# A gated recurrence on one core: the product of z of half B with chunk 0 of h moved in front of the first product with h of half B

## The chip, the cores and the metric

The kernel runs on one core of one Trainium2 chip. The metric is the device time of one execution in microseconds (us). The engines are called as the profile calls them: PE is TensorE with its products, PEld its weight loads, DVE is VectorE, ACT is ScalarE, POOL is GpSimd and SP is SyncE.

## The reference

A recurrence over 512 time steps, for 8 sequences, with a state h of 512 units; x has 512 units per step as well. Cut to what matters:

```python
def step(h, x_t):
    fused = sigmoid(concatenate([x_t, h], axis=-1) @ w_W + w_b)      # 1024 -> 1024
    hidden_state, output_state = split(fused, 2, axis=-1)            # r and z
    memory_state = x_t @ wx_W + wx_b + hidden_state * (h @ wh_W + wh_b)
    h_new = output_state * h + (1.0 - output_state) * tanh(memory_state)
    return (h_new, h_new)
_, hs = scan(step, cond_1024, swapaxes(x, 0, 1))
return x + swapaxes(hs, 0, 1)
```

Everything is float32. In the kernel, r is the gate `hidden_state`, z is the gate `output_state`, "h" is the product of h with `wh_W`, and n is the tanh.

## The kernel before, in words

The 512 units of the state are held as four chunks of 128 partitions by 8 sequences. Chunks 0 and 1 are half A, chunks 2 and 3 half B. The state of half A is in the tiles hTA, that of half B in hTB. Each of them holds a group of 4 steps (GS) in 32 columns, of which the columns of the present step are in use and the others are zero.

What a step multiplies with h is 512x1536 weights: wh, r and z, for 512 outputs each. The outputs lie 32 units (strips, index j) at a time on the partitions of PSUM, as 4 strips of 32 partitions, so that one weight load of TensorE is 128x32 of the state, and the products of the four strips stand beside each other in the array. The columns of the outputs are divided over three banks: A (192 columns: wh, z and r of half A), Z (64 columns: z of half B) and B (128 columns: r and wh of half B). For each bank there are four products, one per chunk k of h, and each is four matmuls (j = 0 to 3). So "A2" is the product of chunk 2 with the columns of bank A. In the trace every matmul stands as two weight loads and two products, 8 of each for an item such as A2. There are two sets of banks, one for the group of 4 steps in work and one for the next. Inside a group the banks gather: the rows of the steps are apart, so each step adds to its own rows.

The order of the items is written out by hand in ORDER (L20) and read in the loop over the 512 steps, just ahead of the rest of a step; the kernel is under a manual schedule there, so each engine works in the order of the text. Products A0, A1, B0, B1, Z0 and Z1 read hTA; A2, A3, B2, B3, Z2 and Z3 read hTB.

After the twelve items of a step comes one item of `prefill`: four matmuls of 384 columns of wx with x of a later group (xp in the profile), which are not part of the recurrence. They go into the bank xp, which is started from the bias by `seed`; ScalarE copies (`spread`, L169) carry it to the banks of the next group in the first and second step of a group, and VectorE turns the part for n (`turn_x`, L172) in the third. The last 8 steps have no such item.

The rest of a step is on VectorE and ScalarE, in this order on VectorE: turn r of half A (`tr`, the first to read bank A, L223), turn wh of half A (`md`, L235), turn z of half A (`tz`, L223), memory of half A (`m`, L252), turn wh of half B (first to read bank B), z times h of half A (`kept`, hd1A, L263), turn r of half B, update of half A (hTA, L275), turn z of half B (`tz` from bank Z), memory of half B, kept of half B, update of half B (hTB). ScalarE makes the sigmoids and tanhs between them (L145). GpSimd adds x to the new state for the output (L308), SyncE issues the loads of x and the stores of the output, one each in 16 steps.

So a step closes on itself in two ways: bank A, then VectorE and ScalarE, then hTA, then A0 of the next step; and bank A, VectorE and ScalarE, hTB, then A2 of the next step.

Of the kernel before, what the change touches and what calls it, by code (L numbers as in the profile page):

```python
# [16 lines left out]
HU = 64  # L17
SYNC = mybir.DependencyInfo(mybir.DependencyClass.Sync, mybir.DependencyReason.DATA)

ORDER = "A0 B0 A1 A2 A3 B1 B2 B3 Z0 Z1 Z2 Z3"  # L20

WH = {"A": slice(0, 192), "Z": slice(192, 256), "B": slice(256, 384)}

# [4 lines left out]
def tile_cond_rnn_residual(  # L28
# [165 lines left out]
    for i in range(T):  # L194
# [8 lines left out]

        for n in ORDER.split():
            bank, k = n[0], int(n[1])
# [175 lines left out]
```

## Time and profile before

| what | value |
|---|---|
| median of 3 runs | 1774.58 us (1774.36 to 1774.95) |
| the profiled execution, its own time | 1775.63 us |
| its span in the trace | 1773.9 us |
| granted TensorE clock | 0.998 |
| busy: PE, PEld, DVE, ACT, POOL | 1751.6, 1422.4, 1129.7, 857.4, 253.4 us |
| instructions in the trace | 121405 |
| products on PE, weight loads on PE | 53312 each |
| product of a bank-A item, mean of one | 327 ns (hTA), 340 ns (hTB) |
| product of a bank-B item, mean of one | 273 ns |
| product of a bank-Z item, mean of one | 223 ns (hTA), 225 ns (hTB) |
| product of the xp item, mean of one | 486 ns |

The means of one product contain its drain, and the products of a strip of four lie over each other, so the time that an item takes from the stream is not the sum of its means. It is read from the starts of the items in the timeline.

The longest waits in the trace are of GpSimd for hTA (1038.0 us in all) and of ScalarE for VectorE's first turn (723.6 us); neither engine is busy for half of the span. The DMA queues moved 31.11 MB in the span, 18 GB/s in the mean.

In the profile's lines, `A<-wh,hTA` is a product into bank A with a weight load from hTA; `128x192 f32 x8` are its partitions, columns, type and the number of instructions that were merged in a line. What stands in square brackets is the idle time of the engine before it and what ended this.

### The profile page before, as it was taken

To read this page: it belongs to the slowest core of one execution; us is meant where nothing else is said; L and a number is where in the kernel's file an instruction comes from. 1 tells how busy PE (TensorE), PEld (TensorE's weight loads), DVE (VectorE), ACT (ScalarE), POOL (GpSimd) and SP (SyncE) were. 2 spreads that over 40 slices of the span, in tenths; PEclk is the share of its full clock that TensorE was granted. 3 is DMA by queue.
4 is the path that set the end of the run, shared out by engine and by line. 5 is a ranking of instruction groups with operands and counts; after the bars stand their busy time and mean duration, and the time that the engine had idled before them with its cause. 6 is when DMAs were issued, how large, how long until landed. Compare 5 with 4: busy or idle time off the path is not lost.

```text
span 1773.9 us, 121405 instructions
## 1 busy us (share of the span) xinstructions
PE 1751.6 (99%) x53312; PEld 1422.4 (80%) x53312; DVE 1129.7 (64%) x6274; ACT 857.4 (48%) x4610; POOL 253.4 (14%) x1053
## 2 busy tenths in 40 slices
PE   7999999999999999999999999999999999999998
PEld 5888888888888888888888888888888888888887
DVE  2666666666666666666666666666666666666665
ACT  2444444444454444444444444444444444444444
POOL 1111111111111111111111111111111111111111
PEclk9999999999999999999999999999999999999999
DMA  4000000000000000000000000000000000000000
GB/s 174 16 4 16 16 16 16 6 15 16 17 16 16 4 16 17 16 16 5 16 16 16 16 15 5 16 16 16 17 4 16 16 16 16 4 16 11 10 10 10
DMA packets 11236, 31.11 MB, mean 18 GB/s; under 512 B 1361, under 2 KB 1361, under 8 KB 10705
## 3 DMA queue, kind: packets, MB, share of 16 engines
q1 hardware_dynamic: 10704, 23.35, 3.9%
q8 instruction: 416, 6.82, 1.6%
q14 instruction: 116, 0.94, 0.2%
HBM read 14.96 MB, written 8.39 MB: 13 GB/s over the span
## 4 chain that ended last, share of the span: by engine, by line
PE 95%; DVE 2%; DMA 1%; ACT 1%; issue 1%; SPq 0%; POOLq 0%; DVEq 0%; POOL 0%; ACTq 0%
PE A L131 40%; PE B L131 24%; PE xp L131 18%; PE Z L131 13%; DMA hin<-in_h_dram 1%; DVE tr L223 1%; DVE hTA L275 0%; ACT md0A L145 0%; DVE m L252 0%; DVE hd1A L263 0%; DMA wx<-in_wx_dram 0%; DVE hTB L275 0%; ACT zB L145 0%; DVE tz L223 0%; DVE md L235 0%
## 5 line engine op out<-in xcount | busy, mean ns | idle before, releaser
L131 PE MATMUL A<-wh,hTA 128*32 128x192 f32 x8192 | 527.1, 327 | 11.2 <-DVE hTB L120 7.4
L145 ACT ACTIVATE md0A<-tr 128x16 f32<-128x16 f32 x512 | 120.9, 236 | 723.6 <-DVE tr L223 723.6
L131 PE MATMUL A<-wh,hTB 128*32 128x192 f32 x8192 | 455.5, 340 | 2.1 <-DVE hTB L275 1.5
L131 PEld LDWEIGHTS A<-wh,hTA 128*32 128x32 f32 x8192 | 275.8, 137 | 220.7 <-DVE hTA L275 212.5
L223 DVE STREAM_TRANSPOSE tr<-A 128x64 f32<-128x64 f32 x512 | 127.9, 250 | 479.9 <-PE A L131 479.9
L131 PE MATMUL xp<-wx,xin 128*32 128x384 f32 x4096 | 425.9, 486 | 0.0
L131 PE MATMUL B<-wh,hTA 128*32 128x128 f32 x8192 | 414.8, 273 | 0.0
L131 PEld LDWEIGHTS A<-wh,hTB 128*32 128x32 f32 x8192 | 273.2, 142 | 105.3 <-DVE hTB L275 98.9
L131 PEld LDWEIGHTS B<-wh,hTA 128*32 128x32 f32 x8192 | 325.2, 136 | 10.3
L131 PE MATMUL B<-wh,hTB 128*32 128x128 f32 x8192 | 318.3, 273 | 0.0
L308 POOL TENSOR_TENSOR ot<-xin,hTA 128x16 f32<-128x16 f32 x512 | 125.8, 246 | 1127.2 <-DVE hTA L275 1038.0
L131 PEld LDWEIGHTS B<-wh,hTB 128*32 128x32 f32 x8192 | 248.3, 136 | 0.0
L131 PE MATMUL Z<-wh,hTB 128*32 128x64 f32 x8192 | 222.6, 225 | 0.0
L131 PE MATMUL Z<-wh,hTA 128*32 128x64 f32 x8192 | 217.2, 223 | 0.0
L131 PEld LDWEIGHTS Z<-wh,hTA 128*32 128x32 f32 x8192 | 200.9, 141 | 0.0
L131 PEld LDWEIGHTS Z<-wh,hTB 128*32 128x32 f32 x8192 | 182.1, 147 | 0.0
L308 POOL TENSOR_TENSOR ot<-xin,hTB 128x16 f32<-128x16 f32 x512 | 124.3, 243 | 389.6 <-DVE hTB L275 389.6
L145 ACT ACTIVATE md0B<-tr 128x16 f32<-128x16 f32 x512 | 119.2, 233 | 108.0 <-DVE tr L223 106.6
L275 DVE TENSOR_TENSOR_SCAN hTB<-hd0B,hd1B 128x32 f32<-128x32 f32 x512 | 115.1, 225 | 55.0 <-DVE hd1B L263 1.0
L235 DVE STREAM_TRANSPOSE md<-B 128x64 f32<-128x64 f32 x512 | 146.7, 286 | 0.6 <-issue 0.5
L235 DVE STREAM_TRANSPOSE md<-A 128x64 f32<-128x64 f32 x512 | 135.8, 265 | 0.0
L252 DVE TENSOR_TENSOR_SCAN m<-md0B,md 128x32 f32<-128x32 f32 x512 | 133.8, 261 | 0.5
(42 smaller groups left out, 1767.3 us busy)
## 6 DMA issues: line engine op xcount, KB each, us to landing
xin<-in_x_dram SPq DMA_DIRECT2D x32, 256.0 KB, 3.0
out_dram<-ot SPq DMA_DIRECT2D x32, 256.0 KB, 2.1
wx<-in_wx_dram SPq DMA_DIRECT2D x4, 768.0 KB, 6.6
wh<-in_wh_dram SPq DMA_DIRECT2D x4, 768.0 KB, 13.5
bias<-in_bias_dram SPq DMA_DIRECT2D x4, 64.0 KB, 2.0
hin<-in_h_dram SPq DMA_DIRECT2D x1, 16.0 KB, 15.0
```

What stands on the lines that cost most here:

```text
L131: nc.tensor.matmul(out_, lhsT, rhs, start=start, stop=False, skip_group_check=True)
L145: inst = nc.scalar.activation(*args, **kw).ins
L223: nc.vector.transpose(t_.rearrange("p c n -> p (c n)"), raw[n][hf])
L235: nc.vector.transpose(md1[g % 2][:, hf, :, :, 0].rearrange("p n c -> p c n"), raw["h"][hf])
L252: nc.vector.tensor_tensor_scan(flat(m), flat(md0[hf][g % 2][:, rows]), flat(md1[g % 2][:, hf, rows]), 0.0, ALU.mult, ALU.add,)
L275: nc.vector.tensor_tensor_scan(flat(hT[hf][(i + 1) % NH][:, B * s1 : B * s1 + B]), flat(hd0[hf][i % 2]), flat(hd1[hf][i % 2]), 0.0, ALU.mu ...
L308: inst = nc.gpsimd.tensor_tensor(ot[:, 2 * hf : 2 * hf + 2, t, :].rearrange("p c n -> p n c"), xins[c][:, 2 * hf : 2 * hf + 2, t * B : t * ...
```

## The change

One line: Z0, the product of chunk 0 of h (half A) with the columns of z of half B, goes from behind B3 to a place in front of A2, the first item that reads hTB.

```diff
-ORDER = "A0 B0 A1 A2 A3 B1 B2 B3 Z0 Z1 Z2 Z3"
+ORDER = "A0 B0 A1 Z0 A2 A3 B1 B2 B3 Z1 Z2 Z3"
```

In the program that is built from it, the four matmuls of Z0 stand between those of A1 and those of A2 in each step. The first of them now carries a wait of its own: for VectorE (its reading of bank Z in the step before) or, in the first step of a group, for ScalarE (its copy into bank Z). Before, VectorE's was contained in the wait of A2. The lists of instructions of VectorE and ScalarE are the same, line by line.

## The prediction

> **What bounds the kernel now.** I read the busy shares first, then the waits, then the timeline of one step, because a busy share near one hides the stalls that matter here. The page's first part says:
>
> ```profile
> PE 1751.6 (99%) x53312; PEld 1422.4 (80%) x53312; DVE 1129.7 (64%) x6274; ACT 857.4 (48%) x4610; POOL 253.4 (14%) x1053
> ```
>
> TensorE looks full. But a product counts as busy while it drains, so the 99% cannot tell a full stream from one with short holes. The view of waits names the holes (who waited, for whom, us in total, times, longest):
>
> ```profile
> DVE tr L223 <- PE A L131: 479.9, 512, 3.3
> PEld A L131 <- DVE hTA L275: 212.5, 509, 1.5
> PEld A L131 <- DVE hTB L275: 98.9, 499, 0.6
> ```
>
> Twice in each of 512 steps a weight load waits for the new state (hTA, then hTB), and VectorE's first turn of a step waits for bank A. So there is a loop through both engines. Which is longer, loop or stream? The timeline of one undisturbed step (start, length, engine):
>
> ```profile
> 903.66 0.83 PE L131 MATMUL xp<-wx,xin 128*32 128x384 f32 x8
> ...
> 904.20 0.27 PEld L131 LDWEIGHTS A<-wh,hTA 128*32 128x32 f32 x8 [0.40 <-DVE hTA L275]
> ...
> 904.30 0.51 PE L131 MATMUL A<-wh,hTA 128*32 128x192 f32 x8
> ...
> 904.63 0.40 PE L131 MATMUL B<-wh,hTA 128*32 128x128 f32 x8
> ...
> 904.85 0.51 PE L131 MATMUL A<-wh,hTA 128*32 128x192 f32 x8
> ...
> 904.92 0.23 DVE L275 TENSOR_TENSOR_SCAN hTB<-hd0B,hd1B 128x32 f32<-128x32 f32 x1
> 905.20 0.54 PEld L131 LDWEIGHTS A<-wh,hTB 128*32 128x32 f32 x16 [0.19 <-DVE hTB L275]
> 905.20 0.89 PE L131 MATMUL A<-wh,hTB 128*32 128x192 f32 x16
> ...
> 905.90 0.40 PE L131 MATMUL B<-wh,hTA 128*32 128x128 f32 x8
> ...
> 906.15 0.25 DVE L223 STREAM_TRANSPOSE tr<-A 128x64 f32<-128x64 f32 x1 [1.01 <-PE A L131]
> ...
> 907.30 0.22 DVE L275 TENSOR_TENSOR_SCAN hTA<-hd0A,hd1A 128x32 f32<-128x32 f32 x1
> 907.44 0.22 DVE L223 STREAM_TRANSPOSE tz<-Z 128x64 f32<-128x64 f32 x1
> 907.58 0.27 PEld L131 LDWEIGHTS A<-wh,hTA 128*32 128x32 f32 x8 [0.40 <-DVE hTA L275]
> ...
> 908.30 0.22 DVE L275 TENSOR_TENSOR_SCAN hTB<-hd0B,hd1B 128x32 f32<-128x32 f32 x1
> ...
> 908.58 0.22 PEld L131 LDWEIGHTS A<-wh,hTB 128*32 128x32 f32 x8 [0.18 <-DVE hTB L275]
> ```
>
> Here is A0 (904.30), B0, A1, then A2 and A3 (905.20), which need hTB, then the B products. A2's load goes from 905.20 to 908.58: 3.38 us, the step. Finer numbers are medians of record starts over steps 100 to 499, in ns.
>
> - **The PE stream.** Unstalled, an A item takes 325, a B item 218, the four Z items 113, 124, 123 and 124, xp 645. Sum 1300+872+484+645 = 3301.
> - **Loop B.** From A2's load to the end of A3's issue 706 (905.20 to 905.90), drain until tr starts 250 (906.15), VectorE and ScalarE until hTB is written 2371 (908.52), then 53 to the load: 3380.
> - **Loop A.** From hTA's end to A0's load 53; A0, B0, A1, A2, A3 on the array 325+218+325+650 = 1518; drain 250; tr to hTA's end 1371 (906.15 to 907.52). A late load also costs its own time: when A2's load comes late, A2 takes 379 to the next item instead of 325, so the array starts about 56 after its load. Sum 53+56+1518+250+1371 = 3248.
>
> The median period is 3383, so loop B binds; the stream has 80 to spare and loop A 132. Cross-check: A1 to A3 starts take 350+379 = 729 instead of 650, a stall of 79, which is the stream's spare time; A0's load stands 110 ahead of its product where 56 would do, 54 more, and 79+54 = 133 is loop A's.
>
> **What the Trainium skill says.** "Perfetto Trace Analysis", Identifying the Most-Contended Engine: matmul busy time is a poor measure, because matmuls are pipelined. The trace agrees: 99% busy over a stall of 79 ns per step. "TensorE: Matmul & The Clock Gate", Step-by-step: what each phase is for: weight loads may be pulled ahead of running products while products stay in order. It agrees: B0's load starts 161 ns ahead of its product. The same page, LDWEIGHTS: a load takes about columns/1.2 ns, 27 ns for 32 columns; the trace shows 56 from a late group of four loads to effective work, and I use 56. "TensorEngine Tiling (Array Packing)", Instruction Overhead: about 60 cycles for any product, so that short ones gain nothing by being shorter. The Z item of 113 to 124 against 218 for twice the columns shows at most a small floor.
>
> **The change, part by part.** Instruction counts, durations and the order on VectorE, ScalarE, GpSimd and SyncE stay; no DMA moves. Four matmuls of 64 columns (eight loads and eight products in the trace) go from after B3 to before A2.
>
> - *Removed behind B3:* one Z item, 118 (113 to 124). From A3's issue to the end of xp it was 654+484+645 = 1783, now 1665. This takes nothing off the time, because A0 will wait for hTA: after A3's issue hTA takes 250+1371, and A0 can start 109 later, at 1730. A pause of 65 opens before A0.
> - *Added before A2:* the same item. It fills the 79 in which the array now waits for hTB. Loop A becomes 3248+118 = 3366 (3361 to 3372), the stream stays 3301, loop B stays 3380: it starts at A2's load, and nothing between there and the next hTB moves relative to it, except that Z1 to Z3 and xp come earlier. The stall goes from the eye but not from the loop: about 14 remain before A2. Cost 0, covered by loop B with 14 ns.
> - *Z's end:* tz of Z comes 118 nearer to being safe. In the waits VectorE never waits for PE there; it follows hTA at once. Gain 0.
> - *An added wait:* Z0 now waits itself for VectorE's tz of the step before (and in the first step of a group for ScalarE's copy). Queued behind it on PE are A2 and all the rest, and VectorE's tr waits for A3. tz ends at 907.66; Z0 comes 868 after 907.69, so the wait has been over for about 0.9 us. A passed wait has no price in the trace: Z0 carried the ScalarE wait in one step of four and came at 2251 there, 2252 in others. I take 0.
> - *Z0's price in its new place* is not shown by the trace, since it always follows B products. Low end 113, the fastest Z item; high end 124+56 = 180, if it or A2 can't have its weights loaded under the product before. I take 118, because A1's second half lasts 162 and covers the load just as B3's 109 does. The high end costs (3248+180-3380) x 511 periods = 24.5 us; the low end can't gain, since loop B doesn't contain the item.
> - *First step:* nothing waits for hTB there, so A3 is 0.12 us later, once.
> - *Late VectorE instructions:* in some 55 places one comes 0.16 to 0.36 us late, 13 us altogether. Both loops pass through VectorE, so such a delay counts once, before and after. Carrying the three sums through all steps with each step's own VectorE times gives 0.1 us more.
>
> Sum: +0.2 us on the profiled execution's 1775.63 (span 1773.9, 1.7 around it): 1775.8. The median of the runs is 1.05 below it, so I say 1774.8.
>
> **The rivals.**
> *Faster: the hTB stall is real time that comes back.* For it: PE at 99%, and a wait of 98.9 us that Z0 covers. Against: loop B has no Z0. Were loop B shorter than it looks (a wait for bank Z in it, which now ends earlier), loop A would bind at 3366: 14 x 511 = 7.2 us, 1767.4. Chance 0.10.
> *Slower: hTA takes over.* Loop A grows past loop B when Z0 costs over 132 in place. Halfway into a reload, 118+28 = 146: 14 x 511 = 7.2 us, 1782.0; fully 1799. For it: the cover is only 14 ns, and A0 is now always late with its load. Against: in the disturbed steps where hTA was late A0 lost only 54, as counted. Chance 0.26.
> *Unchanged: loop B binds before and after.* 1774.8, chance 0.64.
> A measurement of this kernel can tell about 0.2%, 3.5 us, from no change; that is 7 ns per step, so Z0 up to 139 is "same".
>
> **How the numbers follow.** 0.64 within 0.2%, 0.26 slower, 0.10 faster. The forecast's own range is 1773.5 to 1777. The wide one goes down to 1772.5, leaving out most of the faster case (0.08), and up to 1783, where Z0 costs 148, leaving out the worse half of the slower one (0.11).
>
> **What would show it.** If right: A2's load to A2's load stays 3.38 us; A0's record to B0's becomes 379 instead of 325, A0's load just ahead of its product; VectorE's tr to hTB stays 2.37 us; the wait for hTB shrinks well below 98.9 us, although no time is gained; that for hTA grows by some 30 us. If A1 to A2 shows over 325+132, or A2's load comes well after hTB's write, the slower rival holds. If tr to hTB gets shorter than 2.37, the faster one does. The prediction is wrong if bank or memory contention between xp, now 118 ns earlier, and VectorE's turns alters the 2371.

## The result, and the profile after

| kernel | median | ratio to the kernel before on the same chip, 95% interval |
|---|---|---|
| before | 1774.73 us (12 runs) | |
| after | 1773.81 us (12 runs, 1773.11 to 1774.21) | 0.9994 (0.9985 to 1.0003) |

No difference that the measurement can tell. The profiled execution of after took 1773.73 us, its span is 1771.9 us. The first part of its page:

```profile
PE 1747.9 (99%) x53312; PEld 1448.8 (82%) x53312; DVE 1129.2 (64%) x6274; ACT 857.7 (48%) x4610; POOL 253.4 (14%) x1053
```

TensorE is as "full" as before. The waits of after show what moved (who waited, for whom, us in total, times, longest):

```profile
DVE tr L223 <- PE A L131: 478.3, 512, 3.5
...
PEld A L131 <- DVE hTA L275: 275.6, 511, 0.9
...
PEld A L131 <- DVE hTB L275: 2.9, 12, 0.3
```

The wait for hTB went from 98.9 to 2.9 us, and that for hTA from 212.5 to 275.6. VectorE waits for bank A as long as before (479.9 and 478.3). One row has nearly vanished from the view of waits, and the time is the same. The timeline of one step of after (start, length, engine) shows why:

```profile
903.79 0.56 PE L131 MATMUL A<-wh,hTA 128*32 128x192 f32 x8
...
904.17 0.40 PE L131 MATMUL B<-wh,hTA 128*32 128x128 f32 x8
...
904.51 0.23 DVE L275 TENSOR_TENSOR_SCAN hTB<-hd0B,hd1B 128x32 f32<-128x32 f32 x1
904.56 0.32 PEld L131 LDWEIGHTS Z<-wh,hTA 128*32 128x32 f32 x8
904.72 0.29 PE L131 MATMUL Z<-wh,hTA 128*32 128x64 f32 x8
904.79 0.54 PEld L131 LDWEIGHTS A<-wh,hTB 128*32 128x32 f32 x16
...
905.50 0.40 PE L131 MATMUL B<-wh,hTA 128*32 128x128 f32 x8
...
905.75 0.25 DVE L223 STREAM_TRANSPOSE tr<-A 128x64 f32<-128x64 f32 x1 [1.01 <-PE A L131]
...
906.51 0.83 PE L131 MATMUL xp<-wx,xin 128*32 128x384 f32 x8
...
906.89 0.23 DVE L275 TENSOR_TENSOR_SCAN hTA<-hd0A,hd1A 128x32 f32<-128x32 f32 x1
...
907.17 0.22 PEld L131 LDWEIGHTS A<-wh,hTA 128*32 128x32 f32 x8 [0.53 <-DVE hTA L275]
...
908.17 0.54 PEld L131 LDWEIGHTS A<-wh,hTB 128*32 128x32 f32 x16
```

Z0 (904.72) stands where TensorE stood still. A2's load goes from 904.79 to 908.17, 3.38 us, as before. The load follows the end of hTB (904.51+0.23 = 904.74) by 0.05, as before: it still waits for hTB, but the loads of Z0 (904.56, for 0.32 us) now run until past its start, so that the view no longer counts an idle engine. The pause has moved to the front of A0: its load (907.17) came 0.10 ahead of its product before and comes with it now, and A0 takes 0.38 to B0 (903.79 to 904.17) where it took 0.33.

### The profile page after: what moved, and what is told of

It is laid out like the page before. It is cut to its first block, busy times and chain, and to the rows that moved or that the text cites. A ratio compares the mean times of both kernels' runs of the same rounds, so it can differ in the third digit from the quotient of the medians.

```text
span 1771.9 us, 121405 instructions
## 1 busy us (share of the span) xinstructions
PE 1747.9 (99%) x53312; PEld 1448.8 (82%) x53312; DVE 1129.2 (64%) x6274; ACT 857.7 (48%) x4610; POOL 253.4 (14%) x1053
## 4 chain that ended last, share of the span: by engine, by line
PE 94%; DVE 3%; DMA 1%; ACT 1%; issue 1%; SPq 0%; DVEq 0%; POOLq 0%; POOL 0%
PE A L131 40%; PE B L131 24%; PE xp L131 17%; PE Z L131 13%; DMA hin<-in_h_dram 1%; DVE tr L223 1%; DVE hTA L275 1%; ACT md0A L145 0%; DVE m L252 0%; DVE hd1A L263 0%; DMA wx<-in_wx_dram 0%; DVE md L235 0%; DVE hTB L275 0%; DVE tz L223 0%; ACT zB L145 0%
## 5 line engine op out<-in xcount | busy, mean ns | idle before, releaser
L131 PE MATMUL A<-wh,hTA 128*32 128x192 f32 x8192 | 549.3, 340 | 13.5 <-DVE hTB L120 7.5
L131 PEld LDWEIGHTS A<-wh,hTA 128*32 128x32 f32 x8192 | 247.9, 142 | 283.8 <-DVE hTA L275 275.6
L131 PE MATMUL A<-wh,hTB 128*32 128x192 f32 x8192 | 437.6, 331 | 1.4
L223 DVE STREAM_TRANSPOSE tr<-A 128x64 f32<-128x64 f32 x512 | 127.9, 250 | 478.3 <-PE A L131 478.3
L131 PE MATMUL Z<-wh,hTA 128*32 128x64 f32 x8192 | 305.5, 220 | 0.0
L131 PEld LDWEIGHTS Z<-wh,hTA 128*32 128x32 f32 x8192 | 297.1, 136 | 6.0
L235 DVE STREAM_TRANSPOSE md<-B 128x64 f32<-128x64 f32 x512 | 142.9, 279 | 0.6 <-issue 0.6
```

The lines of the kernel that those rows point to most:

```text
L131: nc.tensor.matmul(out_, lhsT, rhs, start=start, stop=False, skip_group_check=True)
L223: nc.vector.transpose(t_.rearrange("p c n -> p (c n)"), raw[n][hf])
L235: nc.vector.transpose(md1[g % 2][:, hf, :, :, 0].rearrange("p n c -> p c n"), raw["h"][hf])
```

## The experiments

The period is the median time from one A0 to the next over steps 100 to 499; other numbers in ns are medians over the same steps. Each ratio is to the kernel before on the same chip. Three readings had to be told apart. *Loop*: the period is the longest of loop A (through hTA), loop B (through hTB) and the PE stream (all products of a step, one behind the other); loop B binds before and after. *Stream*: PE at 99% is full, so order can't matter. *Compensation*: the stall before A2 was real time that the change won, and hTA, now late, gave the same back by chance.

**Two items of Z in front of A2.**

```diff
-ORDER = "A0 B0 A1 A2 A3 B1 B2 B3 Z0 Z1 Z2 Z3"
+ORDER = "A0 B0 A1 Z0 Z1 A2 A3 B1 B2 B3 Z2 Z3"
```

> Z0 and Z1 both stand in front of A2. Loop theory (the period is the longest of loop A through hTA, loop B through hTB, and the PE stream): from the trace after, loop A with Z0 is 325+218+325+113+650 on the array, 251 drain, 1369 to hTA, 54 to the load, 56 for it = 3361 ns; Z1 adds 124, 3485. That is 105 over loop B (3380): 105 x 511 = 53.7 us, so 1828 us (1824 to 1833), and hTB no longer waited for. Stream theory (PE is full, order does not matter): 1774, no change. Compensation theory (hTA already binds after the change, by chance at the old length): +124 x 511 = 63 us, 1837.

Measured: 1831.2 us, ratio 1.0317 (1.0302 to 1.0333). The period is 3491 ns, for 3485 expected. From the waits of this kernel:

```profile
PEld A L131 <- DVE hTA L275: 341.1, 511, 1.2
```

That is 65 us more than in after, and the wait of A2's load for hTB, 2.9 us in after, is down to 0.2. Stream falls: the work on PE is the same and the time is 3% longer. The second Z item cost 113 ns per step (3491 against 3378 in after) of the 124 that it takes.

**Another filler, B1 in front of A2.**

```diff
-ORDER = "A0 B0 A1 A2 A3 B1 B2 B3 Z0 Z1 Z2 Z3"
+ORDER = "A0 B0 A1 B1 A2 A3 B2 B3 Z0 Z1 Z2 Z3"
```

> The order of before with B1, instead of Z0, in front of A2: another filler of 218 ns. Loop theory: loop A 3248+218 = 3466 ns, 86 over loop B; 86 x 511 = 44 us, so 1819 us (1814 to 1822). Stream theory: 1774.7, no change. Compensation theory (the filler takes the 79 ns of stall and gives back what is over 79, then 79 more because A0 is late): anything from +31 to +71 us, 1806 to 1846.

Measured: 1817.82 us, ratio 1.0242 (1.0227 to 1.0257), period 3466 ns. B1 takes 218 ns where loop A had 132 to spare, and 83 more per step are paid, for 86 expected. So it is the length that counts, and not the bank.

**hTB made early, on the order of before.** Half B takes the gates r and z of half A, so that hTB no longer waits for its own; these are computed and not read.

```diff
-                flat(md0[hf][g % 2][:, rows]),
+                flat(md0[0][g % 2][:, rows]),
...
-                zs[hf][i % 2].rearrange("p c n -> p n c"),
+                zs[0][i % 2].rearrange("p c n -> p n c"),
...
-                flat(hd0[hf][i % 2]),
+                flat(hd0[0][i % 2]),
...
-        turn_z(1)
         memory(1)
         kept(1)
+        turn_z(1)
         update(1)
```

> The order of before, but half B takes r and z from half A (its own are still turned and still go through the sigmoid, but nobody reads them, and the turn of z of half B stands behind kept of half B): hTB no longer waits for them. Product and state of half B are therefore not the reference's. All instructions stay, hTA's path stays; hTB comes about 230 ns earlier, loop B 3150. Loop theory: the PE stream binds, 3301 ns, 80 under the period of before: 80 x 511 = 41 us less, and part of the 13 us of late VectorE instructions is covered as well: 1734 us (1722 to 1737). Stream theory: 1774.7, no change, since PE's work is the same.

Measured: 1731.08 us, ratio 0.9754 (0.9738 to 0.977), period 3307 ns. From tr to hTB it is 1997 ns now, 374 less than the 2371 of before (I had expected some 230), and the way from tr to hTA is as before (1370). Still the period stops at 3307: that is the PE stream, estimated at 3301, and no item comes late any more (A0 to B0, A1 to A2 and A2 to A3 are 325 each). The load of A0 still waits for hTA, 206.4 us in all, but it is 101 ns ahead of its product, so this wait costs nothing. PE's page row reads 99% here too:

```profile
PE 1709.7 (99%) x53312; PEld 1493.7 (86%) x53312; DVE 1015.4 (59%) x6274; ACT 904.8 (52%) x4610; POOL 254.1 (15%) x1053
```

The same 53312 products at the same share of the span, 43 us shorter: the 99% of before was not a full stream.

**The same edit on the order of after.** Against the kernel of the experiment above:

```diff
-ORDER = "A0 B0 A1 A2 A3 B1 B2 B3 Z0 Z1 Z2 Z3"
+ORDER = "A0 B0 A1 Z0 A2 A3 B1 B2 B3 Z1 Z2 Z3"
```

> The same edit to the order of after (half B takes r and z from half A, its own are computed and not read). Loop theory: now loop A binds at 3361 ns, only 17 under the period after: 17 x 511 = 9 us less than 1773.8, and a few us of late VectorE instructions after hTA: 1764 us (1758 to 1767), 30 us above the same edit on the order of before. Stream theory: no change, and no difference between the two orders. Compensation theory (hTA binds already after the change): 1773.8, no change, with the order of before at 1734.

Measured: 1763.13 us, ratio 0.9933 (0.9918 to 0.9948), period 3366 ns. Compensation falls: with hTB out of the way after gains 12 ns per step (3378 to 3366), so hTB had been binding in after as well. (The mean gains 19, the time 11 us: the steps with a late VectorE instruction got cheaper too.) And the two orders that are alike by the clock differ by 32 us as soon as loop B is short.

**Without the products of x**, which are left out from the third group on, on the order of before.

```diff
-            pre = prefill(g + 2) if g + 2 < NG else iter(())
+            pre = iter(())
```

> The order of before without the xp items in the loop (the products of x with wx are left out from the third group on, so that only the bias and h's products enter there). PE's stream falls from 3301 to 2656 ns per step. Loop theory: loop B stays 3380 ns and binds, 1774 us (1771 to 1777), with TensorE visibly idle about 0.7 us in each step. Stream theory: 645 x 504 steps = 325 us less, 1450 us; or, if only its 80 ns stall shows, at least 40 us less.

Measured: 1772.01 us, ratio 0.9988 (0.9981 to 0.9995). Its page:

```profile
PE 1564.9 (88%) x49280; PEld 1348.9 (76%) x49280; DVE 1125.6 (64%) x6274; ACT 856.8 (48%) x4610; POOL 252.8 (14%) x1053
```

And the start of a step in its timeline:

```profile
906.01 0.56 PE L131 MATMUL A<-wh,hTA 128*32 128x192 f32 x8 [0.35 <-DVE hTA L275]
```

645 ns of product time taken from each step of 3383 bring 2 us in all; the period is 3375. TensorE's work is not the bound. The 0.7 us of visible idle time that I had expected are 0.35: by the starts of the items the stream has 3375-2656 = 719 ns to spare, but the view counts the last Z product as busy for about 0.2 us after the next item could start, and shows no hole before A2 and behind late loads.

**Z0 elsewhere in front of A2.**

```diff
-ORDER = "A0 B0 A1 A2 A3 B1 B2 B3 Z0 Z1 Z2 Z3"
+ORDER = "A0 Z0 B0 A1 A2 A3 B1 B2 B3 Z1 Z2 Z3"
```

> Z0 directly behind A0 instead of directly ahead of A2: the same items ahead of A2, in another order. Loop theory: loop A is the same sum, 3361 ns, loop B binds, the same time as after, 1773.8 us (1772.5 to 1775.5); it does not matter where in front of A2 the item stands. A theory in which Z0's place next to A2's late load, or its own wait for the turn of z, decides its price: a difference of over 10 ns per step, 5 us, either way.

Measured: 1773.86 us, ratio 0.9998 (0.999 to 1.0007), period 3379 ns for after's 3378. The trace agrees more closely than the time, in which loop B hides up to 12 ns: A0 to A2 is 1042 here and 1035 in after. Within these 7 ns the place and its neighbours don't matter, only what stands ahead of A2.

**The turn of z of half B ahead of the update of half A**, on the order of before.

```diff
+        turn_z(1)
         update(0)
-        turn_z(1)
         memory(1)
```

> The order of before on PE, but on VectorE the turn of z of half B stands ahead of the update of half A: what loop B spends behind hTA is taken ahead of it. Loop theory: hTA comes one turn later, about 142 ns (end of hTA to end of the turn in the trace of before) plus some 19 for which the turn has to wait for Z3; loop A 3248+142+19 = 3409 ns; hTB comes about 95 earlier behind hTA's new place, loop B 3300. Loop A binds, 29 over the old period: 29 x 511 = 15 us more, 1789 us (1779 to 1795), the wait for hTB covered and that for hTA long. A theory in which only the wait for hTB costs time: up to 79 x 511 = 40 us less, 1734 us.

Measured: 1770.03 us, ratio 0.9971 (0.9961 to 0.9982). I had said 1789: a miss, in the price and in the sign. The timeline of the kernel before, around the update of half A:

```profile
907.02 0.18 DVE L263 TENSOR_TENSOR hd1A<-zA,hTA 128x16 f32<-128x16 f32 x1
907.11 0.24 DVE L223 STREAM_TRANSPOSE tr<-B 128x64 f32<-128x64 f32 x1
907.30 0.22 DVE L275 TENSOR_TENSOR_SCAN hTA<-hd0A,hd1A 128x32 f32<-128x32 f32 x1
```

And of this kernel, to the load of A0:

```profile
907.57 0.18 DVE L263 TENSOR_TENSOR hd1A<-zA,hTA 128x16 f32<-128x16 f32 x1
...
907.66 0.24 DVE L223 STREAM_TRANSPOSE tr<-B 128x64 f32<-128x64 f32 x1
907.86 0.25 DVE L223 STREAM_TRANSPOSE tz<-Z 128x64 f32<-128x64 f32 x1
...
908.04 0.18 DVE L275 TENSOR_TENSOR_SCAN hTA<-hd0A,hd1A 128x32 f32<-128x32 f32 x1
...
908.27 0.22 PEld L131 LDWEIGHTS A<-wh,hTA 128*32 128x32 f32 x8 [0.55 <-DVE hTA L275]
```

From tr of half A to the end of hTA it is 1499 ns, 128 more than 1371; I had charged 161. In the kernel before, the update of hTA starts 103 ns after the end of kept of half A, which it reads, and lasts 225. Here the turn of z stands at that place (102 after the end of kept), and the update starts 172 later, but lasts only 182: the charge left out that the update gets shorter behind the turn. So loop A is 1518+251+1499+54+56 = 3378, just under the old 3383, and loop B (tr to hTB now 2249) has 118 to spare. The mean period fell by 11 ns, from 3407 to 3396, of which 5 are in the median; the rest is in the steps with a late VectorE instruction. Why those got cheaper is not shown: room in loop B alone doesn't do it, since with two items of Z in front of A2, where loop B has room as well, the mean stayed 24 above the median, as in before. This kernel is 0.3% faster than before; after was level with it.

**The same order of VectorE with Z0 in front of A2.**

```diff
-ORDER = "A0 B0 A1 A2 A3 B1 B2 B3 Z0 Z1 Z2 Z3"
+ORDER = "A0 B0 A1 Z0 A2 A3 B1 B2 B3 Z1 Z2 Z3"
...
+        turn_z(1)
         update(0)
-        turn_z(1)
         memory(1)
```

> The order of VectorE of the run before (the turn of z of half B ahead of the update of half A) together with the changed order on PE (Z0 in front of A2). There, with Z0 in its old place, hTA's loop was 3378 ns and held a wait of the turn for Z3. Loop theory: with Z0 in front this wait goes (Z3 is through 118 earlier after A3), the turn ends some 51 earlier, but 118 are added ahead of A2: loop A 3378+118-51 = 3445 ns, 67 more per step, 34 us: 1804 us (1797 to 1810). The same edit that cost nothing on the old order of VectorE then costs 34 us. A theory in which Z0 in front of A2 is free by itself: 1770 us.

Measured: 1799.51 us, ratio 1.0135 (1.0118 to 1.0152), period 3435 ns for 3445 expected. The change that is free on the kernel before costs 57 ns per step here (3435 against 3378), because here loop A binds. Z3 comes earlier in this kernel, and the turn behind kept shows it:

```profile
905.41 0.18 DVE L263 TENSOR_TENSOR hd1A<-zA,hTA 128x16 f32<-128x16 f32 x1
905.50 0.24 DVE L223 STREAM_TRANSPOSE tr<-B 128x64 f32<-128x64 f32 x1
905.66 0.21 DVE L223 STREAM_TRANSPOSE tz<-Z 128x64 f32<-128x64 f32 x1
905.80 0.18 DVE L275 TENSOR_TENSOR_SCAN hTA<-hd0A,hd1A 128x32 f32<-128x32 f32 x1
```

The turn starts 82 ns after the end of kept instead of 102, and lasts 207 instead of 250, as it would when its wait for Z3 goes; Z0's place is all that differs between the two kernels. hTA ends 1438 after tr instead of 1499: 61 of the 118 came back, for 51 expected.

## Why the prediction was right

- **Loop B binds and doesn't contain Z0: right, shown.** A2's load to A2's load stayed 3.38 us. The stretch from A2's load to the end of A3's issue is 705 (706 before), the drain (from there until tr can read bank A) 251, from tr to hTB 2368 (2371), to the load 54. The early hTB on the changed order (3366) shows that loop B was still the longest after the change.
- **Loop A grows to 3366, 14 of cover left: right to the nanosecond in one place, within 6 in the other.** With hTB early the changed order runs at 3366; that it fits to the nanosecond is luck, as the terms are off by 1 or 2 each and cancel (Z0 takes 113 and A2 behind it 6 more, for 118; tr to hTA is 1369, for 1371). Cover by that: 12. The second Z item agrees: 124 added, 113 paid, 11 covered.
- **The PE stream of 3301: right, shown** by the early hTB on the order of before, 3307.
- **Z0's price in place: the 113 to 124 hold.** Z0 to A2's record and the 38 that A2's load stands ahead leave a pause of 18 (56-38) for 14 predicted. The dear end of 180 would have shown as 3.43 us per step. The added wait for the turn of z costs nothing: A1 to Z0 is 325, like any A item.
- **A0 late with its load: right.** A0 to B0 is 379 as said, the load 2 ahead of the product. The wait for hTA grew by 63 us, where I had said some 30, and that figure was mis-sized: it took the pause of 65 ns in the products, but the wait is that of the loads. It is counted from the end of xp's loads, which came 123 ns earlier while hTA stayed in its place (401 ns of idle time before A0's load became 524), and 123 x 511 is 63 us.
- **What the rivals rested on:** the faster one saw the vanishing of the hTB row (98.9 to 2.9) as time; it wasn't. The slower one needed a Z0 of over 132; two items or B1 give just that, and cost 56 and 43 us.
- **The sum of +0.2 us** came as -0.9, within the interval of no change. In the trace after, tr to hTB is 3 ns shorter, which is about this size; without the products of x it is 6 shorter (2365). What shortens VectorE's chain by a thousandth when A0 starts late was not tried and stays open.

## What to carry to other kernels

When a wait is hidden by moving other work into it, ask whether the loop that causes the wait contains the moved work: if not, the wait leaves the profile and the time stays. Add up every loop that closes on itself, with its drains and load times, beside the stream of the busiest engine; the longest is the period, and the differences are what an edit may cost before it shows. A neutral edit is not a harmless one: this one used some 120 of 132 ns of slack, and on the kernels with a shorter loop B it cost 32 and 29 us.

## What the runs showed of the hardware

- A busy share of 98 or 99% on TensorE stood for periods from 3307 to 3491 ns with the same 53312 products. What the share can't tell, the spacing of starts can.
- Four weight loads that come late cost their product about 54 to 56 ns: A0 to the next item is 325 when its loads are 101 or more ahead of the product, and 379 when they are 2 ahead, in every kernel here. In between the cost falls step by step: A2 took 18 ns more with its loads 38 ahead (after), 12 with 44 (Z0 behind A0), and 6 with 56 to 60 (hTB early on the changed order, two items of Z).
- An update on VectorE that reads its own engine's earlier result started 103 ns after the end of that one and lasted 225; with a turn between them it lasted 182. So a turn put there delayed the update's end by 128, and by 69 where Z3 came sooner ahead of the turn (1438 against 1369 from tr), while behind the update the turn ended 142 after it.
